# Routing's steps recast, the second search two bits at a time, and unit transposes where TensorE has no operands at the beginning

## The chip, the cores and the metric

The kernel runs on one core of a Trainium2 chip. A core has TensorE (PE: matrix products, with weight loads as a stream of their own, PEld), VectorE (DVE), ScalarE (ACT), GpSimd (POOL) and SyncE (SP, which only issues transfers here). Each works through its own list of instructions in order, and they wait for each other by semaphores. The metric is the device time of one execution in microseconds (us); lower is better.

## The reference

A transformer block with a mixture of experts, in fp32: B = 16 sequences of N = 256 tokens, D = 256, H = 16 heads of 64, E = 8 experts with a hidden size of 1024.

```python
shift = silu(t) @ W_ada.T + b_ada
h = ln(x, ln1_g, ln1_b) + shift
qkv = (h @ Wqkv.T).reshape(b, n, 3, H, HD)
q, k = ln(q, qn_g, qn_b), ln(k, kn_g, kn_b)      # over the 64 of a head
attn = softmax(q @ k.T / sqrt(HD));  o = attn @ v
x = x + o @ Wout.T
tok = x.reshape(-1, d)                           # 4096 tokens
gate = softmax(tok @ Wgate.T, axis=-1)
vals, idx = top_k(gate.T, 4096 // E)             # each expert takes its best 512 tokens
g = ln(tok[idx], mlp_g, mlp_b)
y = gelu(g @ fc1[e].T + b1[e]) @ fc2[e].T + b2[e]
tok = tok.at[idx].add(y * vals)
```

So each expert picks its 512 tokens out of all 4096, which can only be decided when all gates are known.

## The kernel before, in words

**The attention.** Sequences run one after another, overlapped. `First` normalises and transposes the rows of x; `Group` makes one 512-column part of q, k or v for 128 tokens (g 0 and 1 are q, 2 and 3 are k, 4 and 5 are v), with square (ScalarE), sum (VectorE, L628), a power of -1/2 (GpSimd, L82), a scaling (VectorE, L644) and a transposition (TensorE, L653); `Quad` handles four heads; `Tail` projects, adds x, writes `out` and the normalised rows `xn_dram`, and computes the gates. The q and k weights are centred once per head on VectorE (`center`, L531 to L533), so that the mean of q and k need not be taken.

**The order.** Nothing is reordered by a scheduler: every step carries a place, a number in the tables `START`, `STEADY`, `END`, `SEARCH`, `PLACE`, `LIST`, and so on; `at` collects the steps, which are sorted by place and issued in this order. Each engine gets its instructions in that order. The numbers are only positions, not times of the profile.

**The beginning.** SyncE issues x of sequence 0, W_ada and three parts of Wqkv; ScalarE issues the vectors `vec`, the condition `cT`, the gate weights and, at the place `LOADS`, x of sequence 1, the other three parts of Wqkv and Wout. GpSimd makes the constants: the unit matrix `ident`, and for the routing `block`, `twice`, `below`, `ones`, `lane`, `vals`, `gate_of` and `high`.

**The routing.** The gates of an expert are laid as 16 rows of 256 (`turn`, `evict`: `gT`). A threshold is found bit by bit: `compare` counts on VectorE how many gates of a row reach the candidate, a matmul with `block` or `twice` adds the 16 rows of an expert on TensorE, and VectorE decides on the bit. Then `masks`, `totals`, `place` give each chosen token its place among its expert's, and `turn_places`, `split` turn these back and split them in a chunk (0 or 1) and a place below 128. There are two routings. The first takes, from the tokens of the first fifteen sequences, 256 tokens an expert; its 30 rounds (L881, L911, L912, L918, L927) lie between the steps of the last sequence's attention. The second takes the other 256 from all tokens; its 30 rounds (L881, L888, L893, L900) lie between the matmuls of the experts that work on the first list.

**The experts.** There are 16 jobs of 256 tokens: jobs 0 to 7 are the eight experts with the first list, 8 to 15 with the second. A job's list is made by one-hot matrices (`gives`, `onehot`, L1031) and a product (`list_matmul`, L1040), which leaves token numbers and weights (`take`). `gather` fetches the rows of `xn_dram` with two indirect transfers issued by GpSimd (L1059), `transposes` and `evict` turn them, `up` and `gelu`, `down` and `finish` make the result, and `scatter` (L1113) adds it into `out`, again by an indirect transfer issued by GpSimd. Job 0's list, gather and products are in the table of places; from job 1 on there are sixteen slots a job, eight of `up` and eight of `down`. In slot 5 the next job's list, `take` and `gather` are issued, in slot 14 its transposes; the second routing's steps are dealt out one slot each by `second_routing`. Job 0's two scatters are issued with its `down` steps:

```python
at(DOWN[i], partial(jobs[0].down, i), partial(jobs[0].finish, i))
at(DOWN[i][1:], partial(jobs[0].scatter, i))
```

## Time and profile before

| what | value |
|---|---|
| three runs, us | 1196.15, 1191.63, 1195.77; median 1195.77 |
| the profiled execution, us | 1194.45 |
| its span from the first to the last instruction, us | 1192.6 |
| mean granted TensorE clock | 0.992 |
| busy, share of the span | PE 98%, DVE 64%, ACT 52%, POOL 50% |
| DMA | 62.40 MB, mean 52 GB/s |

A row of the profile names a line of the kernel (L1059), an engine, an operation and, as out<-in, the tiles it writes and reads. The bracket at the end of a row in order of time gives how long the engine idled before it and what ended that. Matmuls are pipelined and their ends are modelled, so TensorE's busy time is not time at its peak. The clock is a share of the full TensorE clock; the table of stretches gives it as a mean. Before about 13 us the trace has no clock record and the column shows 1.00; there the length of a weight load tells it.

### The profile page before, as it was taken

What the parts mean: (1) busy time and instruction counts of PE and PEld (TensorE: products, weight loads), DVE (VectorE), ACT (ScalarE), POOL (GpSimd) and SP (SyncE); (2) the same over time, 40 slices, a digit from 0 to 9 for tenths busy, and PEclk for the clock granted to TensorE, in tenths of its full rate; (3) what the DMA queues carried; (4) which work ended last, traced back from release to release, by engine and by line L of the source; (5) the groups of instructions that cost most, each with busy time, mean ns of one, the idle gap of its engine ahead of it and who ended that gap; (6) DMA issues with size and microseconds to landing.
All of it is one profiled execution on the core that took longest, in us unless ns stands there. A gap on an engine that the chain in (4) does not pass through costs nothing. (4 is left out here: it accounts for less than half of the span.)

```text
span 1192.6 us, 19612 instructions
## 1 busy us (share of the span) xinstructions
PE 1162.9 (98%) x6814; PEld 817.1 (69%) x6814; DVE 760.9 (64%) x2274; ACT 624.5 (52%) x1701; POOL 590.7 (50%) x820
## 2 busy tenths in 40 slices
PE   7999999999999999999999999999998989999996
PEld 3566666666676666666666666667755878888885
DVE  7665576666566666666666666565588557865541
ACT  2765655565565656565656566556574422333331
POOL 4665455545555555555554555464674233333332
PEclk9999999999999999999999999999999999999999
DMA  5000000000000000000000000000200446666661
GB/s 187 1 1 5 14 18 19 10 18 10 19 23 5 23 10 19 10 23 6 23 10 28 9 11 14 14 19 19 85 9 1 168 129 186 186 186 185 183 185 22
DMA packets 46738, 62.40 MB, mean 52 GB/s; under 512 B 3888, under 2 KB 39984, under 8 KB 46640
## 3 DMA queue, kind: packets, MB, share of 16 engines
q1 hardware_dynamic: 37680, 49.82, 12.3%
q0 software_dynamic: 6144, 8.39, 3.8%
q10 hardware_dynamic: 2816, 2.95, 0.7%
q8 instruction: 54, 0.88, 0.3%
q14 instruction: 44, 0.36, 0.1%
HBM read 48.56 MB, written 12.58 MB: 51 GB/s over the span
## 5 line engine op out<-in xcount | busy, mean ns | idle before, releaser
L611 PE MATMUL pm<-wq,hT 128*128 128x512 f32 x768 | 365.3, 606 | 2.2 <-ACT qT L665 0.9
L713 POOL TENSOR_SCALAR pr<-pr,sums 128x256 f32<-128x256 f32 x512 | 236.8, 481 | 208.9 <-DVE sums L709 162.2
L82 POOL TENSOR_TENSOR ss<-ss,neghalf 128x8 f32<-128x8 f32 x128 | 211.5, 1653 | 189.8 <-DVE ss L632 185.4
L702 ACT ACTIVATE pr<-sc,nmax 128x256 f32<-128x256 f32 x512 | 236.1, 474 | 116.1 <-DVE nmax L693 111.1
L611 PEld LDWEIGHTS pm<-wq,hT 128*128 128x128 f32 x768 | 134.9, 192 | 126.3 <-issue 112.2
L693 DVE TENSOR_REDUCE nmax<-sc 128x2 f32<-128x512 f32 x256 | 166.5, 683 | 38.3 <-PE sc L686 38.1
L628 DVE TENSOR_REDUCE ss<-sq 128x8 f32<-128x512 f32 x128 | 87.3, 682 | 112.0 <-ACT sq L624 111.5
L722 PEld LDWEIGHTS pp<-ident,pr 128*128 128x128 f32 x1024 | 119.1, 142 | 43.6 <-POOL pr L713 20.3
L722 PE MATMUL pp<-ident,pr 128*128 128x128 f32 x1024 | 139.2, 273 | 0.2
L624 ACT ACTIVATE sq<-pm 128x512 f32<-128x512 f32 x128 | 76.7, 600 | 113.6 <-PE pm L611 107.1
L686 PE MATMUL sc<-kT,qT 64*128 64x256 f32 x1024 | 129.2, 390 | 0.0
L740 PE MATMUL po<-prT,v 128*64 128x256 f32 x1024 | 126.7, 389 | 0.0
L686 PEld LDWEIGHTS sc<-kT,qT 64*128 64x128 f32 x1024 | 93.2, 186 | 40.6 <-issue 30.4
L1103 PE MATMUL py<-w,hid 128*128 128x256 f32 x512 | 118.8, 385 | 0.0
L1087 PE MATMUL ph<-xT,w 128*128 128x256 f32 x512 | 118.4, 384 | 0.0
L764 PE MATMUL pw<-wo,oT 128*128 128x256 f32 x512 | 118.0, 384 | 0.0
L1113 POOL DMA_INDIRECT out<-y,idx x32 | 51.6, 1611 | 123.9 <-DVE y L1110 72.9
L764 PEld LDWEIGHTS pw<-wo,oT 128*128 128x128 f32 x512 | 96.8, 192 | 18.9 <-issue 6.5
L1094 ACT ACTIVATE hid<-ph,vec 128x256 f32<-128x256 f32 x128 | 60.3, 473 | 85.5 <-PE ph L1087 73.4
L1103 PEld LDWEIGHTS py<-w,hid 128*128 128x128 f32 x512 | 95.8, 192 | 13.4
L702 ACT ACTIVATION_READ_ACCUMULATOR pr<-sc,nmax 128x1 f32 x512 | 104.9, 205 | 0.0
L1087 PEld LDWEIGHTS ph<-xT,w 128*128 128x128 f32 x512 | 95.3, 191 | 13.4
(129 smaller groups left out, 1290.7 us busy)
## 6 DMA issues: line engine op xcount, KB each, us to landing
w<-in_fc2T SPq DMA_DIRECT2D x16, 1024.0 KB, 5.6
w<-in_fc1T SPq DMA_DIRECT2D x16, 1024.0 KB, 8.0
out<-tok SPq DMA_DIRECT2D x32, 128.0 KB, 1.7
xn_dram<-tn SPq DMA_DIRECT2D x32, 128.0 KB, 1.7
xs<-in_x SPq DMA_DIRECT2D x15, 256.0 KB, 2.7
b<-in_b2s SPq DMA_DIRECT2D x16, 128.0 KB, 8.2
wq<-in_wqkvT SPq DMA_DIRECT2D x3, 512.0 KB, 6.6
wq<-in_wqkvT ACTq DMA_DIRECT2D x3, 512.0 KB, 6.6
```

What stands on the lines that cost most here:

```text
L82: nc.gpsimd.tensor_tensor(dst, src, neghalf[:, : src.shape[1]], ALU.pow)
L611: nc.tensor.matmul(self.pm, hTs[self.b][:, c, bass.ts(self.t, P)], wq[:, c, bass.ts(self.g, GW)], start=(c == 0), stop=(c == DC - 1),)
L628: nc.vector.tensor_reduce(self.ss[:, 0, :], self.sq.rearrange("p (h d) -> p h d", d=HD), AX.X, ALU.add,)
L686: nc.tensor.matmul(self.sc[i, j][:, t, :], qTs[self.b][rows, hp, bass.ts(t, P)], kTs[self.b][rows, hp, :], start=True, stop=True,)
L693: nc.vector.tensor_reduce(self.nmax[i, j], self.sc[i, j], AX.X, ALU.max, negate=True)
L702: nc.scalar.activation(self.pr[i, j][:, t, :], self.sc[i, j][:, t, :], AF.Exp, bias=self.nmax[i, j][:, t : t + 1], scale=1.0, accum_out=se ...
L713: nc.gpsimd.tensor_scalar(self.pr[i, j][:, t, :], self.pr[i, j][:, t, :], self.sums[i][:, 1, j, t : t + 1], 1.0, ALU.mult, ALU.mult,)
L722: nc.tensor.transpose(self.pp[i, j][:, c, bass.ts(t, P)], self.pr[i, j][:, t, bass.ts(c, P)], ident,)
L740: nc.tensor.matmul(self.po[j * HD : (j + 1) * HD, i, :], vs[self.b][:, c, bass.ts(4 * self.d + 2 * i + j, HD)], self.prT[i, j][:, c, :], s ...
L764: nc.tensor.matmul(self.pw, oTs[self.b][:, hp, bass.ts(self.t, P)], wo[:, hp, :], start=(hp == 0), stop=(hp == HP - 1),)
L1087: nc.tensor.matmul(self.ph[f], self.w1[:, c, bass.ts(f, P)], self.xT[:, c, :], start=(c == 0), stop=(c == DC - 1),)
L1103: nc.tensor.matmul(self.py[i], self.hid[:, f, bass.ts(i, P)], self.w2[:, f, :], start=(f == 0), stop=(f == FC - 1),)
```

## The change

- At the beginning TensorE transposes the unit matrix 40 times, in groups of 16, 4, 8 and 12, before and between its first products (`fill`). `cT` is loaded ahead of `vec`; the scaling `qgb` moves behind the first bias. The parts of Wqkv that ScalarE loads come in the order 5, 1, 3; Wout and x of sequences 2, 3 and 4 are issued by ScalarE later on (`last_loads`), x of 2 to 4 no longer by SyncE. `center` takes two operations instead of three.
- GpSimd makes the routing's constants during sequence 4, in six pieces, with three more (`lane1`, `begin`, `first16`), without `less`.
- The first search starts its counts from `begin` instead of adding a one-row matmul with `less` in every round.
- The second search decides two bits a round: three candidates, three counts, one matmul of three columns, one choice; fifteen rounds, five slots each.
- `scans` are taken out of `place` and start from zero, with the offset added afterwards; `totals` adds up in three matmuls; the two parts of the places are added by TensorE in `turn_places`, four matmuls with the unit matrix instead of two transposes; `split` takes two operations instead of four; `gives` two instead of three, and for job 0 on GpSimd; `take` two instead of three, read from PSUM. Ten of job 0's thirty one-hot tiles are made on ScalarE (two activations each) instead of on GpSimd.
- `finish` takes one operation; the bias times the weight is prepared by `weigh`.
- Job 0's later scatter is issued behind job 2's gather.

```diff
+    cT = const.tile([P, DC, B], F32, name="cT")
+    nc.scalar.dma_start(cT, condT.rearrange("(c p) b -> p c b", p=P))
     vec = const.tile([P, NVEC], F32, name="vec")
     nc.scalar.dma_start(vec, vecs)
-    cT = const.tile([P, DC, B], F32, name="cT")
-    nc.scalar.dma_start(cT, condT.rearrange("(c p) b -> p c b", p=P))
...
+    def make_others():
+        nc.gpsimd.memset(gate_of, -1.0)
+        nc.gpsimd.memset(high, 1 << 29)
+        nc.gpsimd.iota(first16, pattern=[[0, 1]], base=0, channel_multiplier=1)
+        nc.vector.tensor_scalar(first16, first16, 15, None, ALU.bitwise_and)
+        nc.vector.tensor_scalar(begin, first16, 0.0, float(1 - CAPL), ALU.is_equal, ALU.mult)
...
+    FILL = (16, 4, 8, 12)
+    LOADS = (-61.203, -19.863)
...
+        def fill(n):
+            for _ in range(n // 4):
+                pt = ps.tile([P, GW], F32, tag="sc", bufs=4, name="fill")
+                for i in range(4):
+                    nc.tensor.transpose(pt[:, bass.ts(i, P)], ident, ident)
...
         def later_loads():
             load_x(1, nc.scalar)
-            for g in (1, 3, 5):
+            for g in (5, 1, 3):
                 load_wq(g, nc.scalar)
+        def last_loads():
+            load_x(2, nc.scalar)
             nc.scalar.dma_start(wo, woutT.rearrange("(h p) d -> p h d", p=P))
+            for b in (3, 4):
+                load_x(b, nc.scalar)
         def center(g, c):
             w3 = wq[:, c, bass.ts(g, GW)].rearrange("p (h d) -> p h d", d=HD)
             ws = stat.tile([P, 8], F32, tag="ws", name="ws")
             nc.vector.tensor_reduce(ws, w3, AX.X, ALU.add)
-            nc.vector.tensor_scalar_mul(ws, ws, 1.0 / HD)
-            nc.vector.tensor_tensor(
-                w3, w3, ws.unsqueeze(2).to_broadcast([P, 8, HD]), ALU.subtract
+            nc.vector.scalar_tensor_tensor(
+                w3, ws.unsqueeze(2).to_broadcast([P, 8, HD]), -1.0 / HD, w3, ALU.mult, ALU.add
             )
...
+            def compare(self, n, start=None):
                 reach = bit.tile([P, 2 * P], BF16, tag="reach", name="reach")
                 self.cnt = bit.tile([P, 1], BF16, tag="cnt", name="cnt")
                 nc.vector.tensor_scalar(
-                    reach, self.gT, self.cand.bitcast(F32), None, ALU.is_ge, ALU.add,
+                    reach, self.gT, self.cand.bitcast(F32), start, ALU.is_ge, ALU.add,
                     accum_out=self.cnt,
...
+            def candidates(self, n):
+                self.three = bit.tile([P, 3], I32, tag="three", name="three")
+                for k in range(3):
+                    new = self.three[:, k : k + 1]
+                    if n == 28:
+                        nc.vector.memset(new, (k + 1) << n)
+                    else:
+                        nc.vector.tensor_scalar(
+                            new, self.cand, (k + 1) << n, 0, ALU.bitwise_or, ALU.bitwise_or
+                        )
+            def compare_three(self, n):
+                self.cnt = bit.tile([P, 3], BF16, tag="cnt3", name="cnt3")
+                for k in range(3):
+                    reach = bit.tile([P, 2 * P], BF16, tag="reach", name="reach")
+                    nc.vector.tensor_scalar(
+                        reach, self.gT, self.three[:, k : k + 1].bitcast(F32), None,
+                        ALU.is_ge, ALU.add, accum_out=self.cnt[:, k : k + 1],
+                    )
+            def count_three(self, n):
+                self.pc = ps.tile([P, 3], F32, tag="mm", bufs=3, name="pc")
+                nc.tensor.matmul(self.pc, block, self.cnt, start=True, stop=True)
+            def choose_bits(self, n):
+                enough = bit.tile([P, 3], F32, tag="enough", name="enough")
+                many = bit.tile([P, 1], F32, tag="many", name="many")
+                nc.vector.tensor_scalar(
+                    enough, self.pc, CAPL - 0.5, None, ALU.is_ge, ALU.add, accum_out=many
+                )
+                bits = bit.tile([P, 1], I32, tag="bits", name="bits")
+                nc.vector.tensor_scalar(bits, many, float(1 << n), None, ALU.mult)
+                if n == 28:
+                    self.cand = bits
+                else:
+                    old, self.cand = self.cand, bit.tile([P, 1], I32, tag="cand", name="cand")
+                    nc.vector.tensor_tensor(self.cand, old, bits, ALU.bitwise_or)
+            def compare_less(self, n):
+                self.compare(n, begin)
+            def count_over(self, n):
...
-                nc.tensor.matmul(self.pc, ones[:1, :P], less, start=True, stop=False)
-                nc.tensor.matmul(self.pc, twice, self.cnt, start=False, stop=True)
+                nc.tensor.matmul(self.pc, twice, self.cnt, start=True, stop=True)
...
+            def scans(self):
+                self.place_ = route.tile([P, 2, 2 * P], F32, tag="place", name="place")
                 for m in range(2):
                     nc.vector.tensor_tensor_scan(
-                        place[:, m], ones, self.mask[:, m], offset[:, m : m + 1],
-                        ALU.mult, ALU.add,
-                    )
-                nc.vector.tensor_tensor(place, place, self.mask, ALU.mult)
-                nc.vector.tensor_tensor(place[:, 0], place[:, 0], place[:, 1], ALU.add)
-                self.places = place[:, 0]
+                        self.place_[:, m], ones, self.mask[:, m], 0.0, ALU.mult, ALU.add
+                    )
+            def totals(self):
+                self.po = ps.tile([P, 2], F32, tag="mm", bufs=3, name="po")
+                nc.tensor.matmul(self.po[:, :1], below, self.tot[:, :1], start=True, stop=True)
+                nc.tensor.matmul(self.po[:, 1:], below, self.tot[:, 1:], start=True, stop=False)
+                nc.tensor.matmul(self.po[:, 1:], block, self.tot[:, :1], start=False, stop=True)
+            def place(self):
+                offset = route.tile([P, 2], F32, tag="offset", name="offset")
+                nc.vector.tensor_copy(offset, self.po)
+                for m in range(2):
+                    nc.vector.scalar_tensor_tensor(
+                        self.place_[:, m], self.place_[:, m], offset[:, m : m + 1],
+                        self.mask[:, m], ALU.add, ALU.mult,
+                    )
             def turn_places(self):
                 self.pp = ps.tile([P, 2, P], F32, tag="mm", bufs=3, name="pplace")
                 for r in range(2):
-                    nc.tensor.transpose(
-                        self.pp[:, r, :], self.places[:, bass.ts(r, P)], ident
-                    )
+                    for m in range(2):
+                        nc.tensor.matmul(
+                            self.pp[:, r, :], self.place_[:, m, bass.ts(r, P)], ident,
+                            start=(m == 0), stop=(m == 1),
+                        )
...
+                chunk, place = (
+                    self.part[:, k].rearrange("p (k r) -> p r k", r=2) for k in range(2)
+                )
+                nc.vector.tensor_scalar(chunk, self.pp, P + 0.5, None, ALU.is_gt)
+                nc.vector.scalar_tensor_tensor(
+                    place, chunk, -float(P), self.pp, ALU.mult, ALU.add
+                )
...
-            def gives(self):
+            def gives(self, engine=nc.vector):
                 e, n = self.e, self.tiles
-                chunk = moe.tile([P, NT, KL], BF16, tag="chunk", name="chunk")
-                nc.vector.tensor_tensor(
-                    chunk[:, :n],
+                self.give = moe.tile([P, NT, KL, NV], BF16, tag="give", name="give")
+                engine.tensor_tensor(
+                    self.give[:, :n, 1, :], vals[:, e, :n],
                     self.routing.part[:, 0, e * NT : e * NT + n]
-                    .unsqueeze(2).to_broadcast([P, n, KL]),
-                    lane[:, :KL].unsqueeze(1).to_broadcast([P, n, KL]), ALU.is_equal,
-                )
-                self.give = moe.tile([P, NT, KL, NV], BF16, tag="give", name="give")
-                for c in range(KL):
-                    nc.vector.tensor_tensor(
-                        self.give[:, :n, c, :], vals[:, e, :n],
-                        chunk[:, :n, c : c + 1].to_broadcast([P, n, NV]), ALU.mult,
-                    )
+                    .unsqueeze(2).to_broadcast([P, n, NV]), ALU.mult,
+                )
+                engine.tensor_tensor(
+                    self.give[:, :n, 0, :], vals[:, e, :n], self.give[:, :n, 1, :], ALU.subtract
+                )
...
+                    place = self.routing.part[:, 1, k : k + 1]
+                    if engine is nc.scalar:
+                        off = moe.tile([P, P], BF16, tag="off", name="off")
+                        nc.scalar.activation(off, lane1, AF.Abs, bias=place, scale=-1.0)
+                        nc.scalar.activation(self.oh[:, t, :], off, AF.Relu, bias=1.0, scale=-1.0)
+                    else:
+                        nc.vector.tensor_scalar(
+                            self.oh[:, t, :], lane1, place, None, ALU.is_equal
+                        )
...
+                with nc.allow_low_precision(reason="whole numbers below 2 ** 12"):
+                    nc.vector.tensor_reduce(self.idx, self.pls[:, :, :2], AX.X, ALU.add)
                 self.w = moe.tile([P, KL], F32, tag="w", bufs=4, name="w")
-                nc.vector.tensor_reduce(self.w, ls[:, :, 2:], AX.X, ALU.add)
+                nc.vector.tensor_reduce(self.w, self.pls[:, :, 2:], AX.X, ALU.add)
...
+            def weigh(self):
+                self.bw = moe.tile([P, KL, D], F32, tag="bw", name="bw")
+                for i in range(KL):
+                    nc.vector.tensor_scalar_mul(self.bw[:, i], self.b2, self.w[:, i : i + 1])
             def finish(self, i):
-                nc.vector.tensor_tensor(self.y[:, i], self.py[i], self.b2, ALU.add)
-                nc.vector.tensor_scalar_mul(self.y[:, i], self.y[:, i], self.w[:, i : i + 1])
+                nc.vector.scalar_tensor_tensor(
+                    self.y[:, i], self.py[i], self.w[:, i : i + 1], self.bw[:, i],
+                    ALU.mult, ALU.add,
+                )
...
+        for n, p in zip(FILL, (SHIFT[0], max(SHIFT[1][0], SHIFT[2][0]), places(0)["first"][TB][0],
+                         places(0)["group"][4, 0][0])):
+            at([p + 0.001], partial(fill, n))
...
+        for k, f in enumerate((
+            make_block, make_twice, make_lanes, partial(make_vals, 0), partial(make_vals, 1),
+            make_others,
+        )):
+            at([(4 + k / 8) * PERIOD], f)
...
-            at(DOWN[i][1:], partial(jobs[0].scatter, i))
+        at([UP[0][0]], jobs[0].weigh)
+        by_end = sorted(range(KL), key=lambda i: DOWN[i])
+        at(DOWN[by_end[0]][1:], partial(jobs[0].scatter, by_end[0]))
...
+            new = [partial(f, 28) for f in (b.candidates, b.compare_three)]
+            for n in range(28, -1, -2):
+                yield from (new, [], [], [], [])
+                new = [partial(f, n) for f in (b.count_three, b.choose_bits)]
+                new += [partial(f, n - 2) for f in (b.candidates, b.compare_three)] if n else [b.masks, b.scans]
...
+                    if k == 1:
+                        jobs[0].scatter(by_end[1])
```

## The prediction

> **What bounds the kernel now.** I read the page's totals first, then the table by stages, then the waits of TensorE, and only then single stretches in order of time.
>
> ```profile
> span 1192.6 us, 19612 instructions
> PE 1162.9 (98%) x6814; PEld 817.1 (69%) x6814; DVE 760.9 (64%) x2274; ACT 624.5 (52%) x1701; POOL 590.7 (50%) x820
> ...
> 27.00:865.00 838.00, 837.62 (x4817) 555.59 (x4817) 538.51 (x1228) 503.46 (x1429) 456.38 (x666) 1.00 0.05 17
> 865.00:911.00 46.00, 41.28 (x264) 24.99 (x262) 40.38 (x189) 32.47 (x96) 29.52 (x49) 1.00 0.01 4
> 911.00:933.00 22.00, 19.57 (x143) 14.40 (x140) 18.38 (x86) 4.06 (x6) 8.87 (x12) 0.85 0.12 34
> ...
> 961.00:966.00 5.00, 1.54 (x9) 1.06 (x8) 1.60 (x9) 0.40 (x1) 3.38 (x3) 0.95 0.30 62
> 966.00:969.00 3.00, 3.00 (x9) 2.39 (x8) 0.20 (x1) 0.62 (x2) 0.00 (x0) 0.51 0.22 34
> ```
>
> The columns after the stretch are its length, then the busy time of TensorE, its weight loads, VectorE, ScalarE and GpSimd, then the granted clock and DMA. From 27 to 865 us TensorE idles 0.38 us in 838: nothing but less TensorE work helps there, and the change leaves its order there as it was. TensorE loses time only at the beginning, in the first search (865 to 911), at the first list (911 to 933), around 961 to 969 and after the last matmul. Its waits name the causes:
>
> ```profile
> PE pa L499 <- ACT sT L494: 5.1, 1, 5.1
> PE pc L912 <- DVE reach L881: 4.0, 14, 0.5
> PE px L1068 <- DMA xg<-xn_dram,idx: 3.8, 3, 2.6
> PE pls L1040 <- POOL oh L1031: 1.9, 4, 0.5
> ```
>
> **Sum, part by part**, against the profiled execution (1194.45 us, span 1192.6; median of the three runs 1195.77, so it lies 1.3 below).
>
> *Scatter moved behind the gather: -5.1 us, the largest term.* GpSimd issues the scatters and gathers in order:
>
> ```profile
> 949.07 1.67 POOL L1113 DMA_INDIRECT out<-y,idx  x1 [11.43 <-DVE y L1110]
> 957.61 1.57 POOL L1113 DMA_INDIRECT out<-y,idx  x1 [6.87 <-DMA out<-y,idx]
> ...
> 960.71 1.05 POOL L1059 DMA_INDIRECT xg<-xn_dram,idx  x1
> ...
> 963.77 0.30 PE L1068 MATMUL px<-ident,xg 128*128 128x128 f32 x1 [2.57 <-DMA xg<-xn_dram,idx]
> 964.95 0.55 PE L1068 MATMUL px<-ident,xg 128*128 128x128 f32 x3 [0.88 <-DMA xg<-xn_dram,idx]
> ```
>
> Job 0's second scatter stands 6.87 us on GpSimd until the first has landed. Behind it wait five small gate-splitting operations and job 2's two gathers, although idx was written at 953.2. TensorE then idles 2.57 + 0.88 = 3.45 us, and the granted clock falls to half for the next 3.4 us (the row 966 to 969 above shows 0.51), which is half of 3.4 = 1.7 us more. With the scatter behind, GpSimd does the gate parts from 951.4 to 953.4 (1.96 us, as 958.63 to 960.6), and the gathers at about 953.5 and 954.8. A gather takes 2.7 to 5.4 us from issue to landing, so the second lands by 960.2, against 961.2 when TensorE asks. What is late next is the moved scatter: it still waits until 957.6, then job 1's two follow, each behind the landing of the one before; the last leaves GpSimd near 967.6, and job 3's gather is due near 969.7 (974.86 less 5.1), so nothing waits. The margin for the landing is 1 us.
>
> *First search: -1.4 us.* Each of 30 rounds loses a one-row matmul (L911) with its weight load. It starts 0.10 to 0.11 us ahead of the counting matmul where TensorE doesn't wait (897.14 and 897.25). In the 14 rounds that wait for VectorE it lies inside the wait and gives nothing; 16 x 0.105 = 1.7, less about 0.3 where a round then meets VectorE's own loop of some 1.06 us. Ends -1.7 and -0.8.
>
> *First list: +0.5 us.* The place sums are transposed by 4 full fp32 matmuls instead of 2 transposes: an fp32 matmul of 512 columns is two instructions of 0.43 us in the stream, so four of 128 columns are 8 x 0.108 = 0.86 against 2 x 0.11, +0.65. VectorE's work ahead shrinks by 0.6 (scans before the totals; two operations of 0.43 instead of 0.16, 0.69 and 0.42), and `split` from 1.4 to 0.9. So `partf` is ready near 916.5 as before. Ten one-hot tiles then move from GpSimd (6.65 us for ten, 916.57 to 923.2) to ScalarE, two activations each. ScalarE has no such tile in the trace; its SBUF activations took 216 ns for 16 columns and 382 for 224, so 128 columns are about 305 ns, and 20 make 6.1; each pair adds a wait, its neighbours overlap, so 5.5 to 7.1. But they stand behind the copy of oT at 917.5 to 918.1. They end at 923.6 to 925.2, not 923.2. The list product stays the path (TensorE waits for the tiles now too); `take` is one operation shorter to idx (-0.2), and the gather is 0.2 to 1.6 later. Part hides behind L764's 20 matmuls. Ends -0.5 and +1.6; I take +0.5.
>
> *Second search: +0.1 us.* 15 counting matmuls fewer; one costs about 0.07 in the stream (12 matmuls of 0.217 from 958.36 end at 960.96, the next count is at 961.03), -1.0. The second place transposition is +0.65 in full. VectorE gets more: a round of one bit was 0.78 (970.04 to 970.82), two are 1.56; the new pair of bits is three compares of 0.45, three dependent operations of 0.2 and an accumulator read, three candidates of 0.1: 2.3 us at one go, every five slots. That is 0.46 us a slot, against 0.39 in the half of the old search that ran every second slot, where TensorE never idled (969 to 1042: 73.00 of 73). A burst can push `take` or three one-hots back by up to 1.5 us; the gather has 2.7 us in hand (976.17 + 3.3 against 982.24). For the tightest two of the slots +0.5. Ends -0.3 and +2.
>
> *The beginning: -0.7 us.* The rule that speaks against this part: the Trainium skill, TensorE: Matmul & The Clock Gate, "Part 4: PE-mode transpose", says that transposes do not count as busy for the gate, so that the full clock does not engage on them. By it the 24 later unit transposes run cold at 0.22 us and only stand in front of the projections. The trace has a stretch to weigh it with:
>
> ```profile
> 880.00:884.00 4.00, 2.85 (x24) 2.14 (x23) 3.47 (x21) 3.68 (x12) 3.77 (x7) 1.00 0.00 0
> 884.00:887.00 3.00, 2.48 (x21) 1.81 (x20) 2.55 (x15) 1.85 (x3) 2.86 (x5) 1.00 0.03 5
> ```
>
> From 879.66 to 886.12 TensorE ran only 4-transpose groups and one-column matmuls, and the clock stayed at 1.00, then and after. So they count for keeping it; releasing it from cold no row shows. I take the row. Cold, the first 16 run from about 1.6 us (unit matrix ready at 1.52) to 5.1, when `pa` starts anyway (5.08), so they cost nothing. The clock, seen by weight loads 0.33 us long until 12.6 and 0.19 after, is then full several us earlier. But the first projection of wq's centred half waits for VectorE: centring begins at 8.89 with the landing of wq, two pairs of 0.69, without the 0.17 between, end at 11.8 (was 12.03). The 12 transposes in front end near 12.0. The gain is the warm projection: it ended at 14.75 and should end near 14.0; the chain square, sum, power (GpSimd), scale then moves by 0.7, as VectorE's centring lost 0.2 each. What is late next is again PSUM space at 20 to 23 us, with a cold window after it, as now. ScalarE's four added DMA issues there (0.37 to 0.71 each) fall into an idle 3.7 us before the copy at 27.19. By the rule it is instead +1.4. Ends -2.0 and +1.4.
>
> *GpSimd's constants at sequence 4: +0.7 us.* Some 4.5 us leave the beginning, where GpSimd was done at 5.2 before its first power at 5.74: no gain. Between 250 and 283 us four of the six blocks fall into idle GpSimd. `twice`/`below` (0.84) delays two normalised tiles near 259, and the first `vals` (0.83) a power and four tiles near 274; at 276.37 a weight load is released by exactly such a tile. So 0.4 + 0.7, of which I take 0.7. Ends 0 and +2.5. From 27 to 865 there is no idle to pay it from.
>
> *The end: -0.4 us.* The last scatter waited for the one before (1180.44 to 1184.79), and that for VectorE's pair at 1179.36 (0.42 + 0.35 us), now one operation of 0.43: -0.38. `gives`, `weigh` and the loads of x lie beside full TensorE; uncovered, `weigh` would cost 0.7 a job.
>
> Sum: -5.1 - 1.4 + 0.5 + 0.1 - 0.7 + 0.7 - 0.4 = -6.3, so 1188.1 on the profiled execution and 1189.4 on the median. I say 1188.7.
>
> **Rivals.**
> - *The gather lands late all the same.* Its packets follow the first scatter's in one queue and share the engines with the next weights (DMA full from 950 to 956). If it lands at 963.3, 2.1 us of idle and the cold 1.7 stay: +3.8, 1192.5. For: the first scatter took 6.9 us. Against: no gather took over 5.4.
> - *The unit transposes do not release the clock:* +2.1 on the sum, 1190.8.
> - *The ScalarE tiles are slow* (0.4 us each, 926 and a colder list): +2, 1190.7.
> - *Slower: VectorE becomes the bound in the expert stage.* Its bursts of 2.3 us accumulate, and the one-hots of jobs 3 to 7 are late at each list. It needs 1.3 us of TensorE idle in each of five jobs to eat the 6.3; at 2 us a job it is 1198.7, and with a cold window after each up to 1207. For: VectorE was busy 56.3 of 73 us there already. Against: the load per slot above.
>
> **Numbers.** Forecast 0.55, late gather 0.15, cold transposes 0.10, slow tiles 0.06, VectorE 0.14. The likeliest alone is 1184.5 to 1192.5. The range for 8 in 10 is 1183.5 to 1198: low with all terms at their good ends but one, high with VectorE at 2 us a job. A measurement of this kernel can tell about 0.5% (6.0 us) from no change. Under 1189.8 lie seven tenths of the forecast and four tenths of cold and slow tiles: 0.46; over 1201.7 the worse half of VectorE and a rest: 0.10; between: 0.44.
>
> **What would show it.** Right: no wait of px on its DMA near 961 and clock 1.00 there; only weight loads of 0.19 us at 10 us; no L911 rows; list wait on ScalarE near 924; TensorE full through the expert stage. Wrong: px waiting, list products waiting for VectorE's one-hots, new half-clock windows (each is up to 1.7 us, and where they fall is the largest chance in this sum).

## The result, and the profile after

The changed kernel takes 1189.66 us, median of 12 runs (1187.28 to 1194.48), the kernel before 1194.59 us (12 runs, 1191.24 to 1196.17). The ratio is 0.9963, 95% interval 0.9951 to 0.9974: 4.9 us less by the medians. That is inside the 0.5% that the prediction gave as no change, though the interval leaves out 1. The predicted 1188.7 us is 1.0 us off. But of its seven terms one had the wrong sign by 2.3 us and one was not there at all.

The profiled execution of the changed kernel took 1187.28 us, the shortest of its 12, and the one of before 1194.45, near its median, so the two profiles show 7.1 us where the medians show 4.9. Where the half-clock stretches of 3.4 us fall differs from profile to profile, and can make up such a difference.

The totals of the changed kernel:

```profile
span 1185.6 us, 19672 instructions
PE 1157.4 (98%) x6823; PEld 817.5 (69%) x6823; DVE 759.0 (64%) x2303; ACT 630.4 (53%) x1721; POOL 585.4 (49%) x813
```

The same stretches as before, in the same columns (length, TensorE, weight loads, VectorE, ScalarE, GpSimd, granted clock, DMA share, GB/s):

```profile
27.00:865.00 838.00, 837.62 (x4816) 555.12 (x4814) 539.74 (x1234) 502.29 (x1427) 462.87 (x683) 1.00 0.05 17
865.00:911.00 46.00, 37.29 (x232) 22.17 (x232) 41.84 (x184) 31.60 (x94) 27.34 (x45) 0.98 0.01 1
911.00:933.00 22.00, 18.72 (x146) 14.92 (x143) 15.04 (x81) 10.96 (x28) 3.15 (x5) 0.89 0.16 48
961.00:966.00 5.00, 5.00 (x25) 4.33 (x24) 4.41 (x27) 2.21 (x5) 1.57 (x1) 1.00 0.59 116
966.00:969.00 3.00, 3.00 (x41) 2.65 (x40) 2.02 (x12) 1.38 (x3) 2.10 (x2) 1.00 1.07 393
```

From 27 to 865 us nothing has changed, to the hundredth: the constants now made there cost nothing. From 961 to 969 TensorE is full at full clock, where it had 1.54 us of work in 5 and then half a clock. The waits of TensorE (total, times, longest):

```profile
PE pc L956 <- DVE reach L901: 7.1, 16, 0.8
PE pls L1091 <- ACT oh L1081: 3.3, 5, 1.5
...
PE px L1116 <- DMA xg<-xn_dram,idx: 0.8, 1, 0.8
```

The wait of px has gone from 3.8 to 0.8 us, and the 0.8 is an earlier one, at 938 us. But the search waits for VectorE's compare for 7.1 us where it was 4.0, and the list waits 3.3 us for its tiles, on ScalarE, where it was 1.9 on GpSimd. GpSimd's transfers in order of time:

```profile
948.17 1.67 POOL L1168 DMA_INDIRECT out<-y,idx  x1 [11.66 <-DVE gates L844]
952.49 1.03 POOL L1107 DMA_INDIRECT xg<-xn_dram,idx  x1 [0.54 <-DVE idx L1100]
953.82 0.95 POOL L1107 DMA_INDIRECT xg<-xn_dram,idx  x1 [0.30 <-issue]
956.47 1.63 POOL L1168 DMA_INDIRECT out<-y,idx  x1 [1.70 <-DMA out<-y,idx]
```

Both gathers now stand ahead of the second scatter. Between marks that both traces have (starts of TensorE's instructions, and the last end), the span divides so:

| stretch, us | before | after | forecast | measured |
|---|---|---|---|---|
| start to first scores | 31.90 | 29.02 | -0.7 | -2.9 |
| first scores to first transposed gates | 833.80 | 833.79 | +0.7 | 0.0 |
| to the search's first count | 2.16 | 2.08 | | -0.1 |
| first to last count of the first search | 41.21 | 42.07 | -1.4 | +0.9 |
| last count to first list matmul | 11.03 | 11.14 | | +0.1 |
| to the first gathered token's transposition | 9.90 | 10.94 | list +0.5 | +1.0 |
| to the second routing's gates transposed | 23.78 | 23.78 | | 0.0 |
| to the last py matmul | 228.61 | 222.79 | -5.1, +0.1 | -5.8 |
| to the end | 10.26 | 9.95 | -0.4 | -0.3 |

The terms that moved were tried on the chip one by one; the constants and the end were read from the traces alone. All ratios below are to the kernel before.

### The profile page after: what moved, and what is told of

Its sections match the earlier page's. It is cut to its first block, busy times and chain, and to the rows that moved or that the text cites. A ratio compares the mean times of both kernels' runs of the same rounds, so it can differ in the third digit from the quotient of the medians.

```text
span 1185.6 us, 19672 instructions
## 1 busy us (share of the span) xinstructions
PE 1157.4 (98%) x6823; PEld 817.5 (69%) x6823; DVE 759.0 (64%) x2303; ACT 630.4 (53%) x1721; POOL 585.4 (49%) x813
```

## Experiments

### The scatter: back in the changed kernel, alone in the one before

```diff
-        at(DOWN[by_end[0]][1:], partial(jobs[0].scatter, by_end[0]))
+        for i in range(KL):
+            at(DOWN[i][1:], partial(jobs[0].scatter, i))
...
-                    if k == 1:
-                        jobs[0].scatter(by_end[1])
```

> The changed kernel with job 0's second scatter back where it was, ahead of the next job's gather. Theory: the gather of the following job waits on GpSimd behind a scatter that waits for the scatter before it, TensorE then idles some 3.4 us near 963 us and runs the next 3.4 us at half clock, so the whole is 5.1 to 5.4 us longer than the changed kernel: about level with the kernel before (ratio 0.999 to 1.001). Rival (the gather is late anyway, the gain of the changed kernel lies elsewhere): no longer than the changed kernel, ratio 0.996.

Measured: 1196.43 us, ratio 1.0007 (0.9994 to 1.0021). The converse, the kernel before with this edit reversed into it and nothing else:

> The kernel before with the move of job 0's second scatter behind the next gather, and nothing else. Theory: the move alone is worth 5.1 to 5.4 us, ratio 0.9955, as much as the whole change. Rival (the gather is late on its list as well, so the move pays only with the faster list): 0 to 2 us, ratio 0.9985 to 1.000.

Measured: 1188.85 us, ratio 0.9955 (0.9939 to 0.997). GpSimd with the scatter back, in order of time:

```profile
958.29 1.57 POOL L1168 DMA_INDIRECT out<-y,idx  x1 [7.28 <-DMA out<-y,idx]
961.43 1.05 POOL L1107 DMA_INDIRECT xg<-xn_dram,idx  x1
```

and the stages there:

```profile
961.00:966.00 5.00, 1.49 (x7) 0.90 (x6) 2.76 (x18) 0.00 (x0) 3.94 (x5) 0.89 0.30 69
966.00:971.00 5.00, 5.00 (x15) 4.01 (x13) 1.03 (x5) 1.02 (x2) 0.27 (x1) 0.50 0.27 31
```

The whole old picture returns: 7.28 us of GpSimd waiting, TensorE at 1.49 us of 5, then half a clock. Taking the move away costs 0.44%, 5.3 us; making it alone gives 0.45%, 5.4 us. In the profile of the move alone the stretch to the last py matmul is 223.16 us against 228.61, -5.45. The late-gather rival is out. And the move alone is level with the entire change: everything else together comes to about nothing.

### The first search: which of its two edits costs

```diff
-                self.compare(n, begin)
+                self.compare(n)
...
+                nc.tensor.matmul(self.pc, ones[:1, :P], less, start=True, stop=False)
-                nc.tensor.matmul(self.pc, twice, self.cnt, start=True, stop=True)
+                nc.tensor.matmul(self.pc, twice, self.cnt, start=False, stop=True)
```

> The changed kernel with the first search's subtraction back in a matmul of one row, so that VectorE's compare has one pointer scalar and no second. Theory: the compare takes 480 ns again in place of 539 ns, a round of the first search that VectorE sets falls from 1.12 to 1.06 us, and the last count comes 0.8 to 2 us earlier than in the changed kernel (ratio 0.995). Rival (the wider compare hides beside TensorE and the matmul taken out of the chain was worth its 1.4 us): 1 to 1.5 us longer than the changed kernel (ratio 0.997).

Measured: 1188.17 us, ratio 0.9938 (0.992 to 0.9957), and first to last count 41.21 us, the figure of before. That undoes two edits at once. The next run keeps the one-row matmul out and replaces only the pointer by a constant:

```diff
-                self.compare(n, begin)
+                self.compare(n, -16.0)
```

> The changed kernel with a constant, -16, in the first search's compare in place of the pointer to begin: 16 lanes of an expert then take off 256 in place of 255, so the search ends on the value of the 257th token, which the masks and places treat as they treat ties; the rest is the same. Pointer theory (a second scalar read from SBUF costs the compare its 60 ns): compare 480 ns, search's 30 rounds from 42.07 us to 41.2 us or below; without the one-row matmul too it is what the forecast costed (40 to 41 us if the matmul was worth anything, 41.2 if it was hidden). Rival (any starting value makes the counting form slower): compare 539 ns, 42.07 us.

Measured: 1186.94 us, ratio 0.9928 (0.9913 to 0.9943), and 40.52 us from first to last count. VectorE's compare (ns least, median, most) in the kernel before:

```profile
L881 DVE TENSOR_SCALAR_CACHE_REDUCE reach<-gT,cand x29: 465/479/481, 870.2 to 908.5; 128x256 bf16<-128x256 f32 x29
```

in the changed kernel:

```profile
L901 DVE TENSOR_SCALAR_CACHE_REDUCE reach<-gT,cand,begin x29: 523/539/540, 867.3 to 906.4; 128x256 bf16<-128x256 f32 x29
```

and with the constant:

```profile
L901 DVE TENSOR_SCALAR_CACHE_REDUCE reach<-gT,cand x29: 462/479/481, 870.5 to 908.1; 128x256 bf16<-128x256 f32 x29
```

A starting value as a constant is free; as a second pointer it costs 60 ns in each of 30 rounds. 42.07 less 40.52 is 1.55 us, or 0.05 a round: nearly all of the 60 ns reaches the path. The stretch repeats: five profiles with the pointer and no half clock inside it have 42.07 to 42.09 us, three with the constant 40.50 to 40.52. The matmul that was removed is worth 41.21 less 40.52, 0.69 us.

### The first list: ScalarE's tiles

The ten tiles back on GpSimd, the two products on VectorE:

```diff
-                        nc.vector.tensor_scalar(
+                        engine.tensor_scalar(
...
-            at([p["gives"]], partial(a.gives, nc.gpsimd if a is jobs[0] else nc.vector))
+            at([p["gives"]], a.gives)
...
-                engine = nc.scalar if a is jobs[0] and k in (2, 5) else nc.vector
+                engine = nc.gpsimd if a is jobs[0] and k in (2, 5) else nc.vector
```

> The changed kernel with job 0's ten one-hot tiles back on GpSimd and its two products back on VectorE. Theory (the two ScalarE steps of a tile take 0.63 us where GpSimd took one, and this is what the first list lost): the stretch from the last count of the first search to the first transposes of gathered tokens falls from 22.0 us to about 21, the whole is 1 us shorter than the changed kernel (ratio to the kernel before 0.9955). Rival (the list is set by the new place and split steps ahead of it): 22 us as before it, no change (0.996 to 0.997).

Measured: 1188.74 us, ratio 0.9946 (0.9933 to 0.996). From the first list matmul to the first gathered tokens 9.87 us, against 10.94 changed and 9.90 before, each with one half-clock stretch: ScalarE's tiles are the whole 1.0 us. (The stretch named in the expectation fell to 19.4 us, below what was expected; it holds a second half-clock stretch in the changed kernel's profile and not in this one, where 6.8 us at half clock fell into the search instead.) New places and splits gained nothing ahead of the list: 11.03 and 11.14 us, and 9.52 and 9.51 in profiles without a half-clock stretch there.

A tile is not slower on ScalarE. It begins later. Before:

```profile
916.05 0.43 DVE L981 CAST partf<-part 128x512 f32<-128x512 int32 x1
916.57 6.65 POOL L1031 TENSOR_SCALAR oh<-lane,partf 128x128 bf16<-128x128 bf16 x10 [6.00 <-DVE partf L981]
```

and after:

```profile
914.10 0.42 DVE L1025 SCALAR_TENSOR_TENSOR partf<-partf,pplace 128x256 f32<-128x256 f32 x1
915.52 0.58 ACT L770 COPY oT<-po 128x512 f32<-128x512 f32 x1 [2.14 <-PE po L760]
916.00 0.40 ACT L1080 ACTIVATE off<-lane,partf 128x128 bf16<-128x128 bf16 x1
...
922.14 0.31 ACT L1081 ACTIVATE oh<-off 128x128 bf16<-128x128 bf16 x1
```

Ten tiles take 6.65 us on GpSimd and 6.45 on ScalarE. But GpSimd starts 0.1 us after the places (`partf`) are ready, and ScalarE 1.5, behind its copy of oT. So the last tile comes 7.9 us after the places instead of 6.7.

Half of the ten tiles on each engine, ScalarE and VectorE:

```diff
-                engine = nc.scalar if a is jobs[0] and k in (2, 5) else nc.vector
+                engine = nc.scalar if a is jobs[0] and k == 2 else nc.vector
```

> The changed kernel with tiles 25 to 29 of job 0's list on VectorE and only tiles 10 to 14 on ScalarE. Theory (ScalarE's ten tiles at 0.63 us bound the first list, while VectorE stands idle for its last 3 us): TensorE's last wait for a tile ends 1.5 to 2 us earlier, 1.5 to 2 us less than the changed kernel (ratio 0.9945 to 0.995). Rival (the list is awaited for something else, or TensorE's later work at half clock takes the gain): 0 to 0.5 us.

Measured: 1182.91 us, ratio 0.990 (0.9884 to 0.9917), 6.7 us under the changed kernel by the medians (7.5 by the ratios) and much more than expected. TensorE in order of time, changed kernel:

```profile
918.10 0.40 PE L1091 MATMUL pls<-give,oh 128*128 128x10 bf16 x10
919.97 0.18 PE L1091 MATMUL pls<-give,oh 128*128 128x10 bf16 x1 [1.47 <-ACT oh L1081]
...
922.50 0.59 PE L1091 MATMUL pls<-give,oh 128*128 128x10 bf16 x16 [0.45 <-ACT oh L1081]
922.95 1.63 PE L784 MATMUL pw<-wo,oT 128*128 128x256 f32 x3
```

and with the split:

```profile
917.59 0.80 PE L1091 MATMUL pls<-give,oh 128*128 128x10 bf16 x14
918.84 0.56 PE L1091 MATMUL pls<-give,oh 128*128 128x10 bf16 x16 [0.46 <-ACT oh L1081]
919.26 4.56 PE L784 MATMUL pw<-wo,oT 128*128 128x256 f32 x20
```

Of 3.3 us of waits 0.5 is left. A TensorE that doesn't stand idle doesn't lose its clock either: no half-clock stretch follows. First list matmul to gathered tokens is 6.28 us instead of 10.94. The expectation had counted the wait, and not the clock behind it. A further 1.6 us is a half-clock stretch at 908.9 us in the changed kernel's profile (last count to first list matmul 11.14 us against 9.51 with the split). The split does not act there, and other profiles have that stretch or not. Those without it, however, have 6.8 us of half clock behind the list instead of 3.4: in all six profiles with ScalarE's ten tiles and nothing else done to the list, the two stretches together take 21.8 to 22.1 us. In the three with the split they take 15.8. So the split's worth is 6.2 us in these profiles, 4.7 of it in the list itself; that the dip ahead of the list stays away with the split is seen in three profiles and not explained.

To separate wait and clock, unit transposes filled the wait for the tiles, which itself stayed:

```diff
                 for t in range(a, min(b, self.tiles)):
+                    if a == 10 and self.e == 0 and self.routing is first:
+                        for _ in range(6 if t == 10 else 2):
+                            nc.tensor.transpose(self.unit[:, :P], ident, ident)
```

> The changed kernel with fourteen more unit transposes in TensorE's waits for the last tiles of job 0's list (six ahead of tile 10, two ahead of each of tiles 11 to 14, 0.21 us each), which do no work. Clock theory (the 3.41 us at half clock from 922.5 us follow from TensorE standing idle in the 3.41 us before, and cost 1.7 us because TensorE is what the end waits for by then): the dip goes, 1.2 to 1.7 us less than the changed kernel (ratio 0.9945 to 0.9955). Rival (transposes don't count for the clock, as the Trainium skill has it, or the half-clock stretch is hidden behind other waits): level with the changed kernel, or up to 0.5 us longer.

Measured: 1188.32 us, ratio 0.9954 (0.9937 to 0.997), which overlaps the changed kernel's interval. In the profile the effect is plain. Changed kernel, ahead of and behind the end of the list:

```profile
919.00:922.00 3.00, 0.67 (x4) 0.38 (x4) 0.45 (x2) 2.88 (x10) 0.00 (x0) 1.00 0.00 0
922.00:926.00 4.00, 3.55 (x24) 2.95 (x24) 2.87 (x19) 0.42 (x2) 2.10 (x2) 0.57 0.10 28
```

and with transposes in the wait:

```profile
919.00:922.00 3.00, 2.28 (x29) 1.34 (x29) 0.00 (x0) 2.33 (x8) 0.00 (x0) 1.00 0.03 5
922.00:926.00 4.00, 4.00 (x22) 3.54 (x20) 3.89 (x23) 0.00 (x0) 2.23 (x2) 1.00 0.18 48
```

The clock stays at 1.00 and the stretch to the gathered tokens is 9.44 us, 1.50 less. So transposes of a unit matrix keep the clock here: in all ten profiles where the list is waited for and nothing fills the wait, at least 3.4 us of half clock follows. Whether filling helps in every run, the times don't say: they spread over 5.8 us and only the shortest was profiled.

### The second search, one bit at a time again

```diff
...
-            new = [partial(f, 28) for f in (b.candidates, b.compare_three)]
-            for n in range(28, -1, -2):
+            new = [partial(b.compare, 29)]
+            for n in range(29, -1, -1):
...
-                new = [partial(f, n) for f in (b.count_three, b.choose_bits)]
+                new = [partial(f, n) for f in (b.count, b.drop, b.step)]
```

> The changed kernel with the second search back to one bit at a time. Forecast's step (the two-bit search costs 0.1 us, ends -0.3 and +2): level with the changed kernel within 0.3 us. The two profiles' difference (the two-bit search and its shorter tail save 0.5 us in the expert stage by letting the list's tiles come earlier): 0.5 us longer. Rival (45 compares of the search in the place of 30 delay the one-hot tiles): 0.5 to 2 us shorter than the changed kernel.

Measured: 1191.39 us, ratio 0.9959 (0.9945 to 0.9973), not to be told from the changed kernel. In its profile the stretch to the last py matmul is 223.53 us, 0.74 more, where eight profiles with two bits and no late gather have 222.78 to 222.84. With one bit TensorE waits for nothing in this stretch; with two it waits once, 0.36 us for a one-hot tile (at 1029.6 us in the changed kernel), and the stretch is shorter all the same. By the profiles the two-bit search is worth 0.7 us, which the times can't confirm. The VectorE-bound rival is out.

### The unit transposes: left out, and alone in the kernel before

```diff
-    FILL = (16, 4, 8, 12)
+    FILL = (0, 0, 0, 0)
```

> The changed kernel without its forty unit transposes. Theory (they start the full clock 9 us earlier and so hold up most of the 2.9 us gained before the first scores): 1 to 3 us longer than the changed kernel, ratio to the kernel before 0.997 to 0.9985, with a half-clock record up to some 13 us. Rival (the transposes don't move the clock, as the Trainium skill has it for transposes, and the 2.9 us come from the reordered loads and the fused centring): same as the changed kernel, ratio 0.996, and the first scores still near 29 us.

Measured: 1192.66 us, ratio 0.9985 (0.9971 to 1.000), first scores at 31.63 us. The converse adds FILL, its function and its places to the kernel before:

> The kernel before with the forty unit transposes and nothing else. Theory (the transposes are what brings the full clock earlier, worth the 2.6 us that leaving them out cost the changed kernel): 2 to 3 us shorter than the kernel before, ratio 0.9975 to 0.9985. Rival (the matrices of the beginning come too late without the reordered loads and the fused centring, so TensorE waits for them whatever its clock): 0 to 1 us, ratio 0.999 to 1.000.

Measured: 1195.05 us, ratio 1.000 (0.999 to 1.0009), first scores at 32.60 us. These two don't fit a fixed worth of the transposes. The rival of the second is not what its profile shows: TensorE waits for no part of Wqkv there. TensorE's first 15 us show why. Changed kernel:

```profile
1.44 3.36 PE L499 MATMUL fill<-ident 128*128 128x128 f32 x16 [1.44 <-POOL ident masks.py:199]
5.15 1.03 PE L512 MATMUL pa<-sT,wa 128*128 128x16 f32 x8 [0.35 <-DMA wa<-in_w_adaT]
...
6.94 1.04 PE L499 MATMUL fill<-ident 128*128 128x128 f32 x8
7.82 1.93 PE L631 MATMUL pm<-wq,hT 128*128 128x512 f32 x4
```

The changed kernel with the search's matmul back, its beginning the same code:

```profile
1.44 3.68 PE L502 MATMUL fill<-ident 128*128 128x128 f32 x16 [1.44 <-POOL ident masks.py:199]
5.15 1.86 PE L515 MATMUL pa<-sT,wa 128*128 128x16 f32 x8
...
8.59 1.69 PE L502 MATMUL fill<-ident 128*128 128x128 f32 x8
10.12 1.88 PE L634 MATMUL pm<-wq,hT 128*128 128x512 f32 x4
11.84 1.47 PE L502 MATMUL fill<-ident 128*128 128x128 f32 x12
13.14 5.32 PE L634 MATMUL pm<-wq,hT 128*128 128x512 f32 x12
```

In the first the products `pa` take 1.03 us and the eight transposes 1.04; in the second, at the half clock, 1.86 and 1.69. There the transposes stand in front of the projections, which start 2.3 us later. The trace's record of the granted clock starts at full at 4.35 us in the first and 9.91 in the second. Nine profiles have the changed beginning with forty transposes: five are full by 4.4 to 5.9 us and reach their first scores at 28.5 to 30.7 us, four at 9.7 to 10.6 us and reach them at 30.1 to 32.3. Without transposes (three profiles) full starts at 11.9 to 13.6 us and the first scores at 30.1 to 31.9. So released late, they cost as much as they bring; released early, they bring some 1.5 us. A half-clock stretch near 23 us, present in most of these profiles and absent in a few, is worth another 1.6 or so. The mean over the nine is 30.6 us, so the beginning is worth roughly 0.4 to 1 us on average (only three profiles stand against it) and the 2.9 us of the pair of profiles is a good draw.

Why it is early in some runs can be read from the clock records. In each profile all changes of the clock lie on one grid of 3.41 us (the records last 3.41, 6.83, 10.24, 13.65, 17.07 us and so on), and where the grid lies against the kernel's start differs from profile to profile. Eleven profiles have the sixteen first transposes, with this beginning or the old one. In the six with the early clock, the 3.41 us before its start hold 2.63 to 3.04 us of these transposes; in the five with the late clock the grid cuts them, so that no step holds more than 2.51. So the same code is early or late by where the grid happens to lie. What sets that, and whether a longer first group would make it early always, no run here shows.

The 3 us (2.6 by the ratios) that the kernel without transposes lost are not all in the beginning. GpSimd there:

```profile
964.79 1.57 POOL L1168 DMA_INDIRECT out<-y,idx  x1 [3.05 <-DVE reach L922]
974.28 1.55 POOL L1168 DMA_INDIRECT out<-y,idx  x1 [7.91 <-DVE reach L922]
976.14 1.01 POOL L1107 DMA_INDIRECT xg<-xn_dram,idx  x1 [0.30 <-issue]
```

Job 1's second scatter waits 7.91 us and holds up job 3's gather, though idx stood ready at 970.7: the mechanism that the change had removed, one job later. (The bracket names a compare, but the scatter before landed at 973.5 us, and y was ready at 965.8.) It cost 1.4 us of TensorE. In the changed kernel's own profile that scatter left in time (966.60). Of the nine profiles with the move of job 0's scatter alone, this is the only one in which TensorE waits for that gather.

### What is left when the losses are mended

The constant and the split list, both as above, and every job's second scatter behind the next gather:

```diff
...
-                    if k == 1:
-                        jobs[0].scatter(by_end[1])
+                    jobs[k - 1].scatter(by_end[1] if k == 1 else KL - 1)
...
-                        a.scatter(i)
+                        if i < KL - 1 or not new:
+                            a.scatter(i)
```

> The changed kernel with the constant -16 in the first search's compare, tiles 25 to 29 of the first list on VectorE, and every job's second scatter behind the following gather. Theory (three separate stretches, so the gains add): 2.5 us of the search and 6 us of the list below the changed kernel, and up to 1 us of the late gather: 1179.5 to 1182 us, ratio 0.987 to 0.989. Rival (the second takes what the first gave, or held-back scatters come to collide with the next pair): no faster than the list's split alone, 0.990.

Measured: 1181.45 us, ratio 0.9891 (0.9874 to 0.9907). Search 40.52 us, list 6.28: in the profile both gains are there whole. The times alone don't settle it, since 0.9891 is not clear of the split's own 0.990 (1.5 us less by the medians). The scatters bring nothing visible (stretch to the last py matmul 222.79 us, as changed). Then the same with unit transposes in waits:

```diff
...
+                if 30 - n in (3, 4, 5, 8, 9, 10, 11, 12, 13, 19, 20, 25, 26, 27, 28, 29, 30):
+                    nc.tensor.transpose(pc[:, P:], ident, ident)
...
+        for n, g, i in ((3, (2, 0), 0), (4, (2, 1), 0), (4, (0, 0), 5)):
+            at([places(0)["group"][g][i] + 0.001], partial(fill, n))
```

> The same with more unit transposes that do no work: eleven in the waits of the beginning near 17, 20 and 22 us, and one in each of 17 rounds of the first search. Clock theory: the half-clock windows near 23 us and in or after the search no longer come, 1 to 2.5 us less than without them in the median, and the runs lie closer together. Rival (a transpose ahead of the awaited count delays it by up to its 0.21 us in each round): up to 2 us longer.

Measured: 1179.67 us (1178.58 to 1180.28), ratio 0.9873 (0.9854 to 0.9893): 1.8 us less, every run below every run of the one without them, no half-clock stretch left but the one at the very end, and the search not longer (40.50 us). By the medians, here of four runs, it is 15.7 and 10.0 us below the kernel before and the changed one.

## Why the prediction came out near, and where it was wrong

- *Scatter behind the gather, -5.1.* Right, in place, cause and size: 5.3 and 5.4 us in two experiments. px waited no more near 961 us and the clock was 1.00. The chain of scatters did come to hold a gather back in one profile, so "nothing waits" was too sure.
- *First search, -1.4: wrong in sign, +0.9.* The step that failed is the list of what a round loses. It counted the matmul removed and gave the compare's new pointer no cost, in a loop that the same paragraph says VectorE sets at 1.06 us. The pointer costs 1.55 us. The matmul was mis-sized too: 0.69 us, not 1.4. Without it and with the constant TensorE waits 6.8 us in the search against 4.3 before, so most of its time came back as waiting for the other engines.
- *First list, +0.5: measured +1.1,* inside its ends. The tiles were sized well: an activation was taken at 305 ns, the trace has 386 for the one and 309 for the other, which overlap, so a tile comes every 0.63 us, and the late start behind oT was foreseen. The last tile comes 1.2 us later than before, the middle of what was forecast. The step that failed is "part hides behind L764's 20 matmuls": these stand behind the list product in TensorE's order and were late with it (922.95 us is when they start, as soon as the list ends). The step also missed the chance beside it: VectorE stood idle while TensorE waited for ScalarE. Of the slow-tiles rival's 0.4 us an activation one of the two came, of its +2 us about 0.6.
- *Second search, +0.1: about -0.4.* That is 222.79 us against 223.16 for the scatter's move alone, with the place transposition in it; the two bits by themselves give -0.7. VectorE's bursts pushed one list by 0.36 us, near the +0.5 taken for them.
- *Beginning, -0.7: about -0.4 to -1.0 on average,* -2.9 in the profile shown. By the rule weighed there (the Trainium skill, TensorE: Matmul & The Clock Gate, "Part 4: PE-mode transpose": transposes don't count for the gate) it would have been +1.4. This case's traces contradict the rule: in the changed kernel the clock is full at 4.35 us, when only unit transposes had run, and filled waits kept it at 1.00. But the price that stood behind the rule, cold transposes in front of the projections, was paid in four of nine profiles. The forecast took the release as certain once the transposes count; it is not.
- *Constants at sequence 4, +0.7: nothing.* 833.79 us against 833.80. Whatever GpSimd did later there met slack; the single released weight load was no proof that the delays lay on the path.
- *End, -0.4: -0.3.* Right.

So the terms measure -7.1 on the two profiles as they fell and, with the beginning at its mean, about -5, near the medians' -4.9; the sum had -6.3. The forecast was 2.9 us too good for the first search and the list, and some 1.5 too bad for the constants, the second search and the scatter. The number came out nearer still because the kernel before took 1194.59 us in these runs, while 1188.7 and 6.3 make 1195.0. The cause of the gain was right; the nearness of the number is partly luck. Two sums in the prediction are off in the last digit and change nothing: 1195.77 less 6.3 is 1189.5, and the shares below 1189.8 add up to 0.45.

## What to carry to other kernels

An operand that changes from constant to pointer can be an added cost (here 60 ns in a compare of 479); in a serial loop, multiply it by the rounds before counting what the edit saves. On an in-order queue, put what the bottleneck engine awaits ahead of what waits for a landing. Price an idle stretch of TensorE with the half clock that may follow, and fill it either with another engine's free time (here 6 to 7 us for moving five tiles) or, failing that, with transposes that do no work and are not in front of anything awaited.

## What was not expected of the hardware

- The counting compare of 128x256 took 479 ns with one pointer scalar, with or without a constant start, and 539 ns with two pointers.
- On ScalarE a 128x128 bf16 activation took 386 ns with a pointer as bias and 309 ns with a constant (the functions differ, Abs and Relu, so this pair alone doesn't prove the pointer to be the cause).
- The same forty transposes at the start gave full clock by 4.4 to 5.9 us in five profiles and by 9.7 to 10.6 us in four, by where a grid of 3.41 us fell: early where one of its steps held 2.63 us or more of the first sixteen.
- A TensorE that waited 3.3 us in all for the list's tiles ran the next 3.41 us at half clock, worth up to 1.7 us, and transposes in that wait removed it in the profile.
